# Threshold arithmetic in fewer GpSimd operations, two adjacency accumulators and other lags in a planned graph-network kernel

## The chip, the cores and the metric

The kernel runs on one core of a Trainium2 chip. The metric is the device time of one launch in microseconds; lower is better. Five engines work side by side: TensorE (PE in the profile), VectorE (DVE), ScalarE (ACT), GpSimd (POOL) and SyncE (SP), which issues nearly all transfers here.

## The reference, cut to what matters

Two graph layers over N = 3327 nodes with 256 features. Layer 0 makes two steps of two kinds of propagation. `R @ Xf` is a dense product with the row-normalised adjacency. `A @ Xa` uses attention whose rows are cut to the most probable entries that together hold 90% of the probability (top-p).

```python
h = maximum(layernorm(x), 0)                      # layer 0 works on h
R = adj + eye(N); R = R / R.sum(-1, keepdims=True)
Z = 0; Xf = Xa = h
for n in range(2):
    probs = softmax((Xa @ W1.T @ W2.T) @ (Xa @ W3.T).T)
    # keep an entry while the sum of the larger ones in its row is < 0.9
    A = probs * keep;  A = A / A.sum(-1)
    Xf = R @ Xf
    Xa = A @ Xa
    Z = Z + Xf @ U1[n].T + Xa @ U2[n].T
x = x + layernorm(h + Z)
h = maximum(layernorm(x), 0)
# layer 1: graph attention, 4 heads, masked by adj > 0
x = x + elu(softmax(where(adj > 0, leaky_relu(s_i + d_j), -inf)) @ (h @ W))
```

## The kernel before, in words

Nodes are cut into 26 tiles of 128 rows; all work on one tile of rows is a `Row`. Layer 0 is done in two steps, `n` = 0 and 1, and then comes layer 1's attention (`attend_neighbours`).

**One row of attention.** `search` lists its pieces. TensorE computes the logits (line 905), ScalarE their exponentials into a buffer `e` of 128 x 3327 (line 920), one of five. Then the threshold of the row is searched without sorting: ScalarE makes a first guess `t0` (`guess`, `density`, lines 940 to 950) and counts the whole row against it (`count`, line 957, one pass with Relu and one with Sign); GpSimd computes a better threshold from the sums (`step`, lines 965 to 1004), ScalarE counts again, and so on, two evaluations in step 1 and three in step 2 (`EVALS`). All numbers of the search are columns of a small tile `sc`, one number for each of the 128 rows. The last result `up` bounds a window of candidates: VectorE masks the row (line 1014), takes the eight largest of 16 pieces (line 1019), sorts and chooses (`sort`, `choose`), and sets everything under the threshold to zero in four pieces of at most 1024 columns (`drop`, line 1072). `total` on GpSimd gives the reciprocal of the row sum and writes a figure for a later check into `met[:, 4]`.

**From the row to the product.** For most rows VectorE transposes 32 x 32 blocks (line 1110), SyncE writes them to HBM (`put_blocks`) and reads them back in another order (`get_blocks`), and TensorE multiplies them (`attend_blocks`, line 1126). The last 128 columns are transposed by TensorE (`turn`, line 1085) right after the fourth drop. The last three rows of step 2 are all transposed that way (line 1103 is their product). The accumulator is `acca`, one bank of PSUM.

**The adjacency product.** `Full` streams the adjacency in (`load`, `at`), TensorE adds 26 matmuls into the accumulator `accf` (`some`, line 1151), and it is copied out: in step 2 scaled, by ScalarE (line 1162) or VectorE (line 1165).

**What sets the order.** Nothing is scheduled while the kernel runs. Each piece is declared to a planner with `plan.put(engine, length, rank, function, needs, take, give, lag, hold)`: its assumed duration, its priority (lower first), what it waits for, which named buffers it takes and gives back, how long after its end its result may be counted on[...]. `Plan.order` runs through these assumed times once, giving every free engine its ready piece of lowest rank. The program is written down in that order, so each engine's queue is fixed and in order; semaphores follow from the tiles that instructions read and write. An assumed duration or lag that is changed moves instructions on all queues.

Of the kernel before, what the change touches and what calls it, by code (L numbers as in the profile page):

```python
# [10 lines left out]
F32 = mybir.dt.float32  # L11
# [4 lines left out]
ALU = mybir.AluOpType  # L16
# [3 lines left out]
P = 128  # L20
# [567 lines left out]
def fast(  # L588
# [58 lines left out]
    with ExitStack() as l0:  # L647
# [218 lines left out]
        plan = Plan(dict(rows=1, mvs=3, pl=2, px=2, acca=1, accf=1, et=3, at=4, y=1, e2=3, mask=2, e5=1, qg=2, **BUFS))  # L866
# [4 lines left out]
        class Row:  # L871
# [3 lines left out]
                "b v w t0 t1 t2 u g k2 p0 p1 p2 p3 j0 j1 j2 j3 r0 s0 s1 s2 B0 B1 B2 q d dt least up h0 h1 room K zs nxt cnt "  # L875
                "tk rec".split()
# [68 lines left out]
            def density(self):  # L945

                S.activation(self.u, self.w, AF.Square, scale=math.sqrt(0.5))
                S.activation(self.u, self.u, AF.Exp)
                S.activation(self.b, self.s, AF.Copy, scale=1.0 - TOP_P)
                S.activation(self.k2, self.t0, AF.Square, scale=30.0)  # L950
# [8 lines left out]
            def step(self, k, eng):  # L959


                TS, TT = eng.tensor_scalar, eng.tensor_tensor
                t, tn, B = (self.t0, self.t1, self.t2)[k], (self.t1, self.t2, self.up)[k], (self.B0, self.B1, self.B2)[k]
                last = k + 1 == EVALS[self.n]

                def invert(x):
                    if eng is V:
                        V.reciprocal(x, x)
                    else:
                        TT(x, x, powers[:, 2:3], ALU.pow)  # L970

                s = (self.s0, self.s1, self.s2)
                if k == 0:
                    TS(self.q, s[0], float(N), t, ALU.add, ALU.mult)
                    TS(B, self.r0, -2.0, self.q, ALU.mult, ALU.add)
                else:
                    TS(self.v, t, (self.t0, self.t1)[k - 1], 0.5, ALU.add, ALU.mult)
                    TS(self.u, s[k], s[k - 1], self.v, ALU.subtract, ALU.mult)
                    TT(B, (self.B0, self.B1)[k - 1], self.u, ALU.add)
                TS(self.d, B, -0.5, self.b, ALU.mult, ALU.add)  # L980
                if k == self.n:

                    TS(self.least, s[k], N - 2.0 * (WIN[self.n] - 2), BIG, ALU.is_ge, ALU.mult)
                    TS(self.least, self.d, 0.0, self.least, ALU.is_ge, ALU.mult)
                if k == 0:
                    TS(self.g, self.u, cs[:, self.i : self.i + 1], 0.25, ALU.mult, ALU.min)
                elif last:
                    TT(self.w, self.k2, self.g, ALU.mult)
                    TS(self.w, self.u, self.dt, self.w, ALU.mult, ALU.add)
                    TS(self.v, self.u, self.u, self.k2, ALU.mult, ALU.add)  # L990
                    invert(self.v)
                    TT(self.g, self.w, self.v, ALU.mult)
                if k == 0 or last:
                    TS(self.q, self.g, 0.5, 1.0 / AIM[self.n], ALU.mult, ALU.add)
                    invert(self.q)
                TS(self.d, self.q, t, self.d, ALU.mult, ALU.add)
                TT(self.d, self.d, self.g, ALU.mult)
                if last:
                    TS(self.d, self.d, t, self.least, ALU.add, ALU.max)
                    TS(self.up, t, 0.25, self.d, ALU.mult, ALU.max)  # L1000
                else:
                    TT(self.d, self.d, t, ALU.add)
                    TS(tn, t, 0.25, self.d, ALU.mult, ALU.max)  # L1003
                    TS(self.dt, tn, t, 2.0, ALU.subtract, ALU.mult)
# [36 lines left out]
            def choose(self):  # L1041
# [22 lines left out]
                V.scalar_tensor_tensor(num, upto, self.m, num, ALU.is_le, ALU.mult, accum_out=self.tk)  # L1064
# [9 lines left out]
            def total(self):  # L1074

                GP.tensor_scalar(self.v, self.all, self.zs, self.rec, ALU.subtract, ALU.add)
                GP.tensor_tensor(self.rec, self.v, powers[:, 2:3], ALU.pow)
                GP.tensor_tensor(met[:, 4, self.i : self.i + 1], self.tk, self.m, ALU.subtract)
# [56 lines left out]
        class Full:  # L1135
# [11 lines left out]
            def some(self, js):  # L1147
                for j in js:
                    if j == 0:
                        self.acc = ps_a.tile([P, self.w], F32, name="accf")  # L1150
                    T.matmul(  # L1151
                        self.acc[:, : self.w], self.at[j // JC][:, j % JC, :], self.src[:, j, : self.w],
                        start=(j == 0), stop=(j == NT - 1),
                    )
# [35 lines left out]
        ready = []  # L1190
# [288 lines left out]
        def failures(n):  # L1479
# [14 lines left out]
            V.tensor_scalar(one, met[:, 4], 0.0, None, ALU.not_equal)  # L1494
# [7 lines left out]
        def search(row, rank, keys, stats_of, fresh):  # L1502
# [21 lines left out]
            more = plan.put("ACT", 0.55, rank - 2.2, row.density, needs=[a])  # L1524
            for j in range(2):
                got = [
                    plan.put("ACT", 3.05, rank - (2.1, 1.7)[j], row.count, j, fn, needs=[a])
                    for fn in (AF.Relu, AF.Sign)[j:]
                ]
                a = plan.put("POOL", (3.8, (4.7, 3.2)[n])[j], rank - (2.0, 1.6)[j], row.step, j, GP, needs=[got, more])  # L1530
            if EVALS[n] == 3:
                a = row.pieces["counted"] = plan.put("ACT", 3.05, rank - 1.4, row.count, 2, AF.Sign, needs=[a])
                a = plan.put("POOL", 4.3, rank - 1.3, row.step, 2, GP, needs=[a])
# [11 lines left out]
            total = plan.put("POOL", 1.2, rank - 1.0, row.total, needs=[a], give=["cum"])  # L1545
            drops = []
            for o in range(4):
                a = plan.put("DVE", 1.01, rank - 1.0, row.drop, o, needs=[a], hold=1.0)
                drops.append(a)
            return total, drops  # L1550

        def attention(row, rank, total, drops, right):
            a = None
            if row.i < BLOCKED[row.n]:
                come = []
                for g in range(3):
                    b = plan.put("DVE", 1.25, rank - 1.001, row.turn_blocks, g, needs=[drops[g]])
                    b = plan.put("SP", 0.5, rank - 1.0, row.put_blocks, g, needs=[b], lag=6.0)
                    b = plan.put("POOL", 0.02, -90.0, lambda: None, needs=[b], lag=0.0)
                    come.append(  # L1560
                        [plan.put("SP", 0.6, rank - 1.0, row.get_blocks, g, o, needs=[b], lag=4.5) for o in range(4)]
                    )
# [30 lines left out]
        def full(n, t, rank, right, after):  # L1593

            f = Full(n, t)
# [5 lines left out]
            for j in range(0, NT, 2):  # L1601
# [3 lines left out]
                    take=["accf"] * (j == 0), give=["at"] * last,  # L1605
                )
            if n == 1:
                a = plan.either(
                    ("ACT", 0.4, f.scaled_by_s), ("DVE", 0.45, f.scaled_by_v), -90.0, needs=[a], give=["accf"]
                )  # L1610
                b = plan.put("SP", 0.4, rank, f.fetch, needs=[loads[-1], stored[t]], take=["base"], lag=3.0)
# [497 lines left out]
```

## Time and profile before

| what | us |
|---|---|
| median of 3 runs | 2116.03 |
| lowest, highest | 2112.54, 2118.37 |
| profiled execution, its own time | 2116.11 |
| its span, first to last instruction | 2114.3 |
| TensorE busy in the span | 2044.3 |
| VectorE, ScalarE, GpSimd busy | 1732.8, 1285.1, 1073.9 |

The profile is of one execution. A name such as `PE accf L1151` is an engine, the tile written and the line of the kernel. A line of the waits, `A <- B: 9.6, 7, 3.7`, says that A stood still for B for 9.6 us in all, 7 times, at most 3.7 us at once. A group of instructions shows, after its shapes, how often it ran, its busy time and the mean of one in ns, and then the idle time ahead of it. A matmul of 32-bit numbers leaves two records in the trace, each 0.216 us apart for 256 columns.

### The profile page before, as it was taken

What the parts mean: (1) busy time and instruction counts of PE and PEld (TensorE: products, weight loads), DVE (VectorE), ACT (ScalarE), POOL (GpSimd) and SP (SyncE); (2) the same over time, 40 slices, a digit from 0 to 9 for tenths busy, and PEclk for the clock granted to TensorE, in tenths of its full rate; (3) what the DMA queues carried; (4) which work ended last, traced back from release to release, by engine and by line L of the source; (5) the groups of instructions that cost most, each with busy time, mean ns of one, the idle gap of its engine ahead of it and who ended that gap; (6) DMA issues with size and microseconds to landing.
All of it is one profiled execution on the core that took longest, in us unless ns stands there. A gap on an engine that the chain in (4) does not pass through costs nothing. (4 is left out here: it accounts for less than half of the span.)

```text
span 2114.3 us, 34595 instructions
## 1 busy us (share of the span) xinstructions
PE 2044.3 (97%) x10695; PEld 1414.4 (67%) x10695; DVE 1732.8 (82%) x4110; ACT 1285.1 (61%) x2371; POOL 1073.9 (51%) x2482
## 2 busy tenths in 40 slices
PE   8999999999999999999999999999999999999997
PEld 6477877877877888777777877878777333333332
DVE  5577998878887971569888989979787999999895
ACT  5676665566566612678677777767653547464552
POOL 4366675546565620568878888888883000000001
PEclk9999999999999999999999999999999999999999
DMA  3177978788876994787777887868763544454341
GB/s 96 44 187 176 194 194 193 168 170 183 188 177 166 205 207 129 217 182 181 182 177 166 190 194 177 199 158 198 160 153 91 165 140 140 119 153 117 110 127 34
DMA packets 580514, 338.57 MB, mean 160 GB/s; under 512 B 327930, under 2 KB 533280, under 8 KB 580320
## 3 DMA queue, kind: packets, MB, share of 16 engines
q1 hardware_dynamic: 579424, 336.06, 65.5%
q8 instruction: 87, 1.43, 0.3%
q14 instruction: 107, 0.88, 0.1%
q10 hardware_dynamic: 896, 0.21, 0.0%
HBM read 242.86 MB, written 93.05 MB: 159 GB/s over the span
## 5 line engine op out<-in xcount | busy, mean ns | idle before, releaser
L957 ACT ACTIVATE junk<-e,sc 128x3327 fp8e5<-128x3327 f32 x147 | 450.7, 3066 | 66.0 <-POOL sc L1003 64.5
L1126 PE MATMUL acca<-rhs,e 128*128 128x256 f32 x1872 | 423.9, 380 | 7.9 <-DMA e<-blocks 7.3
L1126 PEld LDWEIGHTS acca<-rhs,e 128*128 128x128 f32 x1872 | 364.1, 196 | 52.2 <-issue 13.0
L1151 PE MATMUL accf<-c,at 128*128 128x256 f32 x1352 | 318.9, 387 | 18.2 <-ACT main L1162 9.6
L1151 PE MATMUL accf<-main,at 128*128 128x257 f32 x1352 | 318.5, 384 | 6.2 <-DVE win L1036 4.0
L1151 PEld LDWEIGHTS accf<-c,at 128*128 128x128 f32 x1352 | 253.5, 192 | 70.0 <-ACT main L1162 12.4
L1151 PEld LDWEIGHTS accf<-main,at 128*128 128x128 f32 x1352 | 251.9, 191 | 59.2 <-issue 12.3
L1019 DVE MAX8 cands<-y 128x8 f32<-128x205 f32 (+1 forms) x832 | 243.1, 362 | 3.6
L1909 POOL TENSOR_TENSOR qq<-qq 128x256 f32<-128x256 f32 x4 | 3.0, 768 | 457.1 <-ACT qq L1905 457.0
L1014 DVE SCALAR_TENSOR_TENSOR y<-e,sc 128x1639 f32<-128x1639 f32 x84 | 165.1, 1965 | 57.6 <-POOL sc L1000 56.4
L1743 ACT ACTIVATE et<-at 128x448 bf16<-128x448 f32 (+1 forms) x204 | 112.2, 550 | 129.5 <-DVE e L1754 73.7
L1770 PE MATMUL pl<-e,main 128*64 128x416 f32 x1024 | 190.4, 517 | 0.1
L920 ACT ACTIVATE e<-pl 128x1024 f32<-128x1024 f32 (+1 forms) x168 | 152.0, 916 | 53.1 <-PE pl L905 51.5
L1072 DVE SCALAR_TENSOR_TENSOR e<-e,thr 128x1024 f32<-128x1024 f32 (+1 forms) x168 | 178.6, 1066 | 3.0 <-DMA kqs<-kq 0.5
L905 PE MATMUL pl<-kt,qg 64*128 64x512 f32 (+1 forms) x832 | 173.8, 536 | 0.0
L1110 DVE STREAM_TRANSPOSE e<-e 128x1024 f32<-128x1024 f32 x117 | 145.9, 1247 | 3.6
L1770 PEld LDWEIGHTS pl<-e,main 128*64 128x64 f32 x1024 | 70.3, 137 | 111.1 <-issue 92.2
L1754 DVE SCALAR_TENSOR_TENSOR e<-c,low,et 128x832 f32<-128x832 f32 x128 | 128.8, 1073 | 6.1 <-issue 3.2
L905 PEld LDWEIGHTS pl<-kt,qg 64*128 64x128 f32 x832 | 71.8, 186 | 83.9 <-issue 75.2
L1742 ACT ACTIVATE at<-at 128x448 f32<-128x448 f32 (+1 forms) x204 | 110.5, 541 | 25.3 <-DMA at<-in_adjt_dram 25.2
L1754 DVE SCALAR_TENSOR_TENSOR e<-qq,low,et 128x832 f32<-128x832 f32 x120 | 120.7, 1084 | 4.1 <-PE accf L1784 2.8
L957 ACT ACTIVATE junk<-qq,sc 128x3327 fp8e5<-128x3327 f32 x35 | 107.3, 3064 | 24.9 <-POOL sc L1003 24.8
(545 smaller groups left out, 3600.2 us busy)
## 6 DMA issues: line engine op xcount, KB each, us to landing
at<-in_adjt_dram SPq DMA_DIRECT2D x414, 256.0 KB
blocks<-e SPq DMA_DIRECT2D x117, 512.0 KB
e<-blocks SPq DMA_DIRECT2D x468, 128.0 KB
at<-in_adjt_dram SPq DMA_DIRECT2D x102, 192.0 KB
blocks<-qq SPq DMA_DIRECT2D x30, 512.0 KB
qq<-blocks SPq DMA_DIRECT2D x120, 128.0 KB
at<-in_adjt_dram SPq DMA_DIRECT2D x52, 128.0 KB
ys<-ystage SPq DMA_DIRECT2D x26, 256.0 KB
```

The lines of the kernel that those rows point to most:

```text
L905: T.matmul(pl[:, lo : lo + m], qg[self.n, self.i // 4][half, self.i % 4, :], kt[half, 512 * k : 512 * k + m], start=True, stop=True,)
L920: S.activation(to, pl, AF.Exp, accum_out=(self.p0, self.p1, self.p2, self.p3)[k],)
L957: S.activation(junk[:, :N], self.e[:, :N], fn, bias=t, scale=-1.0, accum_out=dst, saturate=False)
L1014: V.scalar_tensor_tensor(self.y[:, : hi - lo], self.e[:, lo:hi], self.up, self.e[:, lo:hi], ALU.is_lt, ALU.mult, accum_out=(self.h0, self. ...
L1019: V.max(self.cands[:, a * PIECES // 2 + k, :], self.y[:, at[k] - lo : at[k + 1] - lo])
L1072: V.scalar_tensor_tensor(piece, piece, self.thr[:, o : o + 1], piece, ALU.is_gt, ALU.mult)
L1110: V.transpose(part, part)
L1126: T.matmul(self.acc, lhs, rhs[self.n][:, j, :], start=(j == 0), stop=stop and j == js[-1])
L1151: T.matmul(self.acc[:, : self.w], self.at[j // JC][:, j % JC, :], self.src[:, j, : self.w], start=(j == 0), stop=(j == NT - 1),)
L1743: S.activation(to, src, AF.Sign)
L1754: V.scalar_tensor_tensor(held["e"][:, k, :], extra["both"][b % 2][:, k, :], low[:, j, k : k + 1], held["mask"], ALU.max, ALU.mult,)
L1770: T.matmul(q["acc"][a][k * FH : (k + 1) * FH, c, :C], main[:, j, h * FH : (h + 1) * FH], held["e"][:, h, c * C : (c + 1) * C], start=(j == 0),
```

## The change

`step(k)` is split. `before(k)` computes on GpSimd what doesn't need the count that is running (`g`, `h`, `x`, `mid`, floors of the result); `step(k)` does the rest. Halves and signs are moved into constants, so that some operations fall away, ScalarE makes two more small ones in `density` (`th`, `tq`), and the two reciprocals of the last evaluation are one operation on two neighbouring columns `v`, `z`. The comparison that `total` made for each row is made once for all rows in `failures`. The pieces get other assumed lengths.

In step 2 the adjacency accumulator becomes one tile of 512 columns, of which even and odd tiles of rows use a half each; the planner is told of two buffers, `fa` and `fb`.

For the planner the first three drops last 1.07 us and the fourth 0.4 (before 1.01 each), what follows the fourth may come 1.5 us after it (before 0.15), and blocks read back are counted on after 5.5 us (before 4.5).

```diff
             def density(self):
...
-                S.activation(self.k2, self.t0, AF.Square, scale=30.0)
+                S.activation(self.k2, self.t0, AF.Square, scale=15.0)
+                S.activation(self.th, self.t0, AF.Copy, scale=-0.5)
+                S.activation(self.tq, self.t0, AF.Copy, scale=0.25)
...
-            def step(self, k, eng):
...
-                if k == 0:
-                    TS(self.q, s[0], float(N), t, ALU.add, ALU.mult)
-                    TS(B, self.r0, -2.0, self.q, ALU.mult, ALU.add)
-                else:
-                    TS(self.v, t, (self.t0, self.t1)[k - 1], 0.5, ALU.add, ALU.mult)
-                    TS(self.u, s[k], s[k - 1], self.v, ALU.subtract, ALU.mult)
-                    TT(B, (self.B0, self.B1)[k - 1], self.u, ALU.add)
-                TS(self.d, B, -0.5, self.b, ALU.mult, ALU.add)
-                if k == self.n:
...
-                    TS(self.least, s[k], N - 2.0 * (WIN[self.n] - 2), BIG, ALU.is_ge, ALU.mult)
-                    TS(self.least, self.d, 0.0, self.least, ALU.is_ge, ALU.mult)
+            def before(self, k):
...
                 if k == 0:
                     TS(self.g, self.u, cs[:, self.i : self.i + 1], 0.25, ALU.mult, ALU.min)
-                elif last:
-                    TT(self.w, self.k2, self.g, ALU.mult)
-                    TS(self.w, self.u, self.dt, self.w, ALU.mult, ALU.add)
+                    TS(self.h, self.g, 0.5, 1.0 / A, ALU.mult, ALU.add)
+                    TT(self.h, self.h, powers[:, 2:3], ALU.pow)
+                    TT(self.x, self.h, t, ALU.mult)
+                    return
+                TS(self.mid, t, ts[k - 1], -0.25, ALU.add, ALU.mult)
+                if k + 1 < EVALS[n]:
+                    TT(self.x, self.h, t, ALU.mult)
+                    TS(self.tq, t, 0.25, None, ALU.mult)
+                else:
+                    TS(self.dh, ts[k - 1], t, 0.5, ALU.subtract, ALU.mult)
+                    TS(self.kh, self.k2, self.g, 0.5, ALU.mult, ALU.mult)
+                    TS(self.fl, ss[n], N - 2.0 * (WIN[n] - 2), BIG, ALU.is_ge, ALU.mult)
+                    TS(self.fl, Ds[n], 0.0, self.fl, ALU.is_ge, ALU.mult)
+                    TS(self.fl, t, 0.25, self.fl, ALU.mult, ALU.max)
+
+            def step(self, k):
...
+                if k == 0:
+                    TS(self.mid, s[0], float(N), self.th, ALU.add, ALU.mult)
+                    TS(D, self.mid, self.r0, self.b, ALU.add, ALU.add)
+                else:
+                    TS(self.u, s[k], s[k - 1], self.mid, ALU.subtract, ALU.mult)
+                    TT(D, (self.D0, self.D1)[k - 1], self.u, ALU.add)
+                if k + 1 < EVALS[self.n]:
+                    TS(d, D, self.x, self.g, ALU.add, ALU.mult)
+                    TS((self.t1, self.t2)[k], d, t, self.tq, ALU.add, ALU.max)
+                else:
                     TS(self.v, self.u, self.u, self.k2, ALU.mult, ALU.add)
-                    invert(self.v)
-                    TT(self.g, self.w, self.v, ALU.mult)
-                if k == 0 or last:
-                    TS(self.q, self.g, 0.5, 1.0 / AIM[self.n], ALU.mult, ALU.add)
-                    invert(self.q)
-                TS(self.d, self.q, t, self.d, ALU.mult, ALU.add)
-                TT(self.d, self.d, self.g, ALU.mult)
-                if last:
-                    TS(self.d, self.d, t, self.least, ALU.add, ALU.max)
-                    TS(self.up, t, 0.25, self.d, ALU.mult, ALU.max)
-                else:
-                    TT(self.d, self.d, t, ALU.add)
-                    TS(tn, t, 0.25, self.d, ALU.mult, ALU.max)
-                    TS(self.dt, tn, t, 2.0, ALU.subtract, ALU.mult)
+                    TS(self.w, self.u, self.dh, self.kh, ALU.mult, ALU.add)
+                    TS(self.z, self.v, 1.0 / A, self.w, ALU.mult, ALU.add)
+                    k = self.NAMES.index("v")
+                    both = self.sc[:, k : k + 2]
+                    TT(both, both, powers[:, 2:3].to_broadcast([P, 2]), ALU.pow)
+                    TT(self.x, t, self.z, ALU.mult)
+                    TS(d, D, self.v, self.x, ALU.mult, ALU.add)
+                    TS(d, d, self.w, 2.0, ALU.mult, ALU.mult)
+                    TS(self.up, d, t, self.fl, ALU.add, ALU.max)
...
             def total(self):
...
-                GP.tensor_tensor(met[:, 4, self.i : self.i + 1], self.tk, self.m, ALU.subtract)
...
             def some(self, js):
                 for j in js:
                     if j == 0:
-                        self.acc = ps_a.tile([P, self.w], F32, name="accf")
+                        if self.n == 0 or self.t == 0:
+                            pair[0] = ps_a.tile([P, 512], F32, name="accf")
+                        lo = 0 if self.n == 0 else self.t % 2 * D
+                        self.acc = pair[0][:, lo : lo + self.w]
...
-            more = plan.put("ACT", 0.55, rank - 2.2, row.density, needs=[a])
-            for j in range(2):
-                got = [
-                    plan.put("ACT", 3.05, rank - (2.1, 1.7)[j], row.count, j, fn, needs=[a])
-                    for fn in (AF.Relu, AF.Sign)[j:]
+            more = plan.put("ACT", 0.95, rank - 2.2, row.density, needs=[a])
+            b = plan.put("POOL", 1.7, rank - 2.0, row.before, 0, needs=[more])
+            last = EVALS[n] - 1
+            for j in range(last + 1):
+                r = rank - (2.0, 1.6, 1.3)[j]
+                a = [
+                    plan.put("ACT", 3.05, r - 0.1, row.count, j, fn, needs=[a])
+                    for fn in ((AF.Relu, AF.Sign) if j == 0 else (AF.Sign,))
                 ]
-                a = plan.put("POOL", (3.8, (4.7, 3.2)[n])[j], rank - (2.0, 1.6)[j], row.step, j, GP, needs=[got, more])
-            if EVALS[n] == 3:
-                a = row.pieces["counted"] = plan.put("ACT", 3.05, rank - 1.4, row.count, 2, AF.Sign, needs=[a])
-                a = plan.put("POOL", 4.3, rank - 1.3, row.step, 2, GP, needs=[a])
+                if j == 2:
+                    row.pieces["counted"] = a
+                a = plan.put("POOL", 1.55 if j < last else 4.1, r, row.step, j, needs=[a, b])
+                if j < last:
+                    b = plan.put("POOL", 2.3 if j + 1 == last else 1.15, r + 0.1, row.before, j + 1, needs=[a])
...
-            total = plan.put("POOL", 1.2, rank - 1.0, row.total, needs=[a], give=["cum"])
+            total = plan.put("POOL", 1.0, rank - 1.0, row.total, needs=[a], give=["cum"])
             drops = []
             for o in range(4):
-                a = plan.put("DVE", 1.01, rank - 1.0, row.drop, o, needs=[a], hold=1.0)
+                a = plan.put(
+                    "DVE", 1.07 if o < 3 else 0.4, rank - 1.0, row.drop, o, needs=[a], hold=1.0 if o < 3 else 0.3,
+                    lag=0.15 if o < 3 else 1.5,
+                )
                 drops.append(a)
...
-                        [plan.put("SP", 0.6, rank - 1.0, row.get_blocks, g, o, needs=[b], lag=4.5) for o in range(4)]
+                        [plan.put("SP", 0.6, rank - 1.0, row.get_blocks, g, o, needs=[b], lag=5.5) for o in range(4)]
...
-            f = Full(n, t)
+            f, mine = Full(n, t), ["accf"] if n == 0 else [("fa", "fb")[t % 2]]
...
-                    take=["accf"] * (j == 0), give=["at"] * last,
+                    take=mine * (j == 0) + ["accf"] * (n == 1 and t == j == 0), give=["at"] * last,
...
             if n == 1:
                 a = plan.either(
-                    ("ACT", 0.4, f.scaled_by_s), ("DVE", 0.45, f.scaled_by_v), -90.0, needs=[a], give=["accf"]
+                    ("ACT", 0.4, f.scaled_by_s), ("DVE", 0.45, f.scaled_by_v), -90.0, needs=[a], give=mine
                 )
```

## The prediction

> **What bounds the kernel now.** The page comes first: its busy line tells which engine has no room left.
>
> ```profile
> span 2114.3 us, 34595 instructions
> ...
> PE 2044.3 (97%) x10695; PEld 1414.4 (67%) x10695; DVE 1732.8 (82%) x4110; ACT 1285.1 (61%) x2371; POOL 1073.9 (51%) x2482
> ```
>
> TensorE is the bound, so the time is its work plus its idle time, 2114.3 - 2044.3 = 70.0 us. Its matmuls are the same after the change (5585 TensorE instructions in both built programs), so only those 70 us can move. The table by windows says where they lie: step 1 is about 95 to 860 us, step 2 860 to 1610, the layer-1 attention the rest.
>
> ```profile
> 860.00:1610.00 750.00, 710.85 (x3294) 568.25 (x3291) 641.32 (x1759) 523.15 (x849) 592.24 (x1346) 0.99 0.76 179
> 95.00:860.00 765.00, 755.45 (x3485) 601.80 (x3487) 591.86 (x1635) 444.04 (x757) 423.82 (x984) 1.00 0.78 180
> ```
>
> The second column is TensorE: it idles 750 - 710.85 = 39.2 us in step 2 and 9.6 us in step 1; some 21 us lie in the start and the last stage, which the diff hardly touches. GpSimd (the sixth) is 79% busy in step 2 and 55% in step 1. So the change is worth what it does to 39 us, and the waits of TensorE between 860 and 1610 us name them (total, times, longest):
>
> ```profile
> PE accf L1151 <- ACT main L1162: 9.6, 7, 3.7
> PE px L1085 <- DVE e L1072: 7.8, 8, 2.1
> PE acca L1126 <- DMA e<-blocks: 7.3, 10, 1.5
> PE accf L1151 <- DMA at<-in_adjt_dram: 5.6, 3, 3.8
> PE accf L1151 <- DVE main L1165: 3.0, 2, 2.4
> ```
>
> These five are 33.3 us. The change aims at four of them: the finished adj accumulator being copied out (9.6 + 3.0 = 12.6 us in 9 waits), the last drop before a transpose (7.8), and blocks coming back from HBM (7.3). Only the adjacency load (5.6) is not addressed. Two more waits in the same window show how threshold arithmetic reaches the others: ScalarE's counts and VectorE's windows wait for its last operation.
>
> ```profile
> ACT junk L957 <- POOL sc L1003: 48.5, 27, 6.9
> ...
> DVE y L1014 <- POOL sc L1000: 41.2, 11, 7.9
> ```
>
> Neither engine is full, so these cost time only where they make a copy or a drop late.
>
> [...] operations on one number per partition take 0.3 to 0.6 us, so on GpSimd the number of instructions is the cost.
>
> **Part 1, the arithmetic.** Three groups carry the prices (mean ns of one after the busy time):
>
> ```profile
> L970 POOL TENSOR_TENSOR sc<-sc,powers 128x1 f32<-128x1 f32 x156 | 98.2, 629 | 13.0
> L996 POOL TENSOR_SCALAR sc<-sc 128x1 f32<-128x1 f32 x130 | 68.4, 526 | 13.9
> ...
> L980 POOL TENSOR_SCALAR sc<-sc 128x1 f32<-128x1 f32 x130 | 42.2, 324 | 13.6
> ```
>
> In step 2 a row has 11, 11 and 15 operations after its three counts. Adding the means of their lines in that window gives 4.25 + 4.33 + 6.26 = 14.8 us; the planner assumed 3.8 + 3.2 + 4.3 = 11.3. After, 4 + 4 + 10 operations follow a count, by the same rows 1.6 + 1.7 + 4.5 = 7.8 us, and 4 + 3 + 6 run while ScalarE counts (3.07 us a count): 1.5 + 1.1 + 2.4 = 5.0. Together 12.8 us, where the new plan assumes 12.35. The power of two numbers at once is not in the trace; 0.63 us for one and 0.99 for four (L851) bound it, and I take 0.75. GpSimd has 312 instructions fewer in all (2170 for 2482, one for each row in `total`), about 62 us less in step 2 and 45 in step 1. TensorE gets none of this directly. What it gets is a plan whose order is off by 0.4 us a row on GpSimd instead of 3.5, so ScalarE and VectorE keep their places better. I take 2 us in step 2 (an eighth of the 12.6 us of copies that come late), between 0 and 8, and 1 us in step 1.
>
> ScalarE pays two operations more a row at 0.19 us (as L949 and L950), 52 x 0.38 = 20 us. They stand ahead of the row's counts, which start 0.4 us later; ScalarE is idle 227 of 750 us in step 2, so I cost them at nothing. Without that cover they would come behind copies TensorE waits for, at most 10 us in step 2.
>
> **Part 2, two accumulators.** Both halves are columns of one tile in one bank, and the built order shows what becomes of that. In 16 of 25 changes of tile, matmuls of the next tile (mostly a pair of blocks) now stand before the copy of the finished one. But the copy waits for that pair, and the pair after it waits for the copy: the wait is not gone, it has moved 0.87 us into the next tile (4 records of 0.216 us). Counting what stands on TensorE between the matmul that releases the copy and the one that waits for it: nothing in 9 cases before and in 10 after; in 5 more of after only two to four small matmuls or transposes. Queued behind the waiting matmul is everything on TensorE, logits of the next rows too. Before, a bare change cost 12.6 / 9 = 1.4 us. After, the copy itself (0.47 us) is the least a bare one can cost; but a ScalarE that comes late has 0.87 us of grace. I take 0.9 us for ten and 0.3 for five: 10.5 us, **2 us less** than 12.6. The ends are 10 x 0.47 = 4.7 us (8 less) and 15 x 1.4 = 21 us (8 more).
>
> **Part 3, later drops and loads.** No instruction is added. The plan gives the drops 3 x 1.07 + 0.4 us and then 1.5 us before the last transpose may follow, 5.1 us; before it was 4 x 1.01 + 0.15 = 4.2. The trace has 1.25 us for each of the three large drops and 0.44 for the small one, 4.2 us. So transposes move 0.9 us later behind other matmuls, against waits of 1.0 us on average and 2.1 at most: if these spread evenly from 0 to 2.1 us, (1.2 / 2.1) squared = a third is left. **5 us less** of 7.8. The block loads are assumed 1.0 us later, against waits of 0.7 on average and 1.5 at most: by the same reckoning a tenth is left, **6 us less** of 7.3, if the queue of SP, which issues puts, block loads and adjacency loads in one order, does not fall behind. The 468 + 120 block loads move later in it, past adjacency loads, which come no later for it. A row keeps its buffer 1 us longer of some 144 (five buffers, 28.8 us a row), which costs nothing. What is late next is the adjacency load, 5.6 us.
>
> **The sum.** A new order makes waits of its own; I allow 3 us (nothing to 10). Then -2 - 1 - 2 - 5 - 6 + 3 = -13 us. The profiled execution took 2116.1 us around its span of 2114.3, as good as the median of 2116.0. **2103 us.**
>
> **The rivals.** *No change, about 2113 us.* VectorE is 641 of 750 us busy in step 2, and the plan believes in 3.6 us of drops where the trace has 4.2. It falls behind 0.6 us a row, where it was 0.16, and eats the 0.9 us given. Then parts 1 to 3 leave some 3 us. For it: `DVE y <- POOL`, which shows it waiting already. Against: these waits shrink with 7 us less arithmetic on a row's path.
>
> *Slower, about 2128 us.* The copies. A copy on ScalarE stands in line behind counts of 3.07 us, and now TensorE has already been committed to the next tile when it finds out. At 2.4 us for each of the 15 thinly covered changes they cost 36 us instead of 12.6, +23, and the rest of the sum, without the 2 of part 2, is -11: +12. This decides from some 1.6 us a change (24 us, 11 more than before: the rest's gain is used up). For it: the longest copy wait of 3.7 us. Against: the 1.4 us average, and a ScalarE less often held by GpSimd.
>
> *Much faster, about 2091 us.* With threshold operations off the path, all four addressed waits go almost entirely: 12.6 + 7.8 + 7.3 = 27.7, less 3 for new ones. For it: the waits of 48.5 and 41.2 us. [...] That the change does not do what it says holds for its second part, by the built order, and is in the sum already.
>
> **How the numbers follow.** About 0.3%, 6.3 us, is what a measurement of this kernel can tell from no change. The forecast has 0.47, much faster 0.13, no change 0.20, slower 0.20. Faster is 0.60, same 0.20, slower 0.20. The range runs from 2086 us (all 27.7 us of the addressed idle time gone, and 2 of the rest) to 2126 (15 x 2.25 = 34 us of copy waits, 21 more, against -11).
>
> **What would show it.** GpSimd busy near 960 us; TensorE idle in step 2 near 27 us; the waits for L1072 and for blocks together under 5 us; waits of adj matmuls for the copies still there, around 10 us, but in the middle of a tile. It is wrong if the copy waits are gone or above 20 us, if transposes still wait 7 us for drops, or if step 1 loses what step 2 gains.

## The result, and the profile after

The changed kernel takes as long as the one before: 2114.53 us against 2113.88 (medians of 12 runs each), ratio 0.9999 with a 95% interval of 0.999 to 1.0008. The forecast was 2103. The profiled execution took 2113.02 us around a span of 2111.2.

The busy line of the page after, with its span:

```profile
span 2111.2 us, 34313 instructions
...
PE 2041.5 (97%) x10695; PEld 1414.9 (67%) x10695; DVE 1728.0 (82%) x4108; ACT 1297.9 (61%) x2477; POOL 993.5 (47%) x2170
```

GpSimd works 80 us less. TensorE idles 2111.2 - 2041.5 = 69.7 us, where it was 70.0. The table by windows of the changed kernel, step 2 and then step 1 (sum, then TensorE, its weight loads, VectorE, ScalarE, GpSimd, granted clock, DMA share, GB/s):

```profile
860.00:1610.00 750.00, 717.21 (x3323) 577.00 (x3322) 640.82 (x1761) 530.70 (x901) 544.24 (x1174) 0.99 0.77 180
95.00:860.00 765.00, 749.71 (x3462) 596.45 (x3463) 587.02 (x1617) 446.59 (x806) 391.61 (x845) 1.00 0.78 179
```

Idle time of TensorE in step 2 fell from 39.2 to 32.8 us, and in step 1 it rose from 9.6 to 15.3. Nearly all that step 2 gained, step 1 lost. The waits of TensorE in step 2 of the changed kernel (total, times, longest; L1156 is the adj matmul, L1087 the transpose after the fourth drop, L1128 the product of blocks):

```profile
PE accf L1156 <- DMA at<-in_adjt_dram: 9.2, 6, 4.5
PE px L1087 <- ACT et L1098: 5.4, 1, 5.4
PE accf L1156 <- ACT main L1167: 4.5, 8, 0.6
PE pl L905 <- ACT e L920: 3.1, 1, 3.1
PE acca L1128 <- DMA e<-blocks: 2.7, 5, 0.8
PE accf L1156 <- DVE main L1170: 2.3, 4, 1.0
PE px L1087 <- DVE e L1075: 2.1, 3, 0.9
```

The waits that the change aims at did fall: copies 4.5 + 2.3 = 6.8 us (12.6 before), drops 2.1 (7.8), blocks 2.7 (7.3), together 11.6 for 27.7. None of them is over 1 us at once any more. But other single waits stand high in the list: one of 5.4, one of 3.1, and loads of up to 4.5. A fourth heads the waits of step 1 (95 to 860 us):

```profile
PE px L1087 <- ACT ystage L1350: 7.7, 2, 6.8
```

The two longest, of 6.8 and 5.4 us, can be followed to a transfer. At 740.3 us VectorE writes the last part of a `ystage` tile; SyncE issues its store only at 743.7, behind twelve block loads and four adjacency loads, and ScalarE can't overwrite the tile until the store has landed, at 751.2. That copy would have freed the PSUM tile that TensorE's transpose needs. Who waited for whom is in the answer for the tile `ystage`, 725 to 756 us:

```profile
L1361 SPq DMA_DIRECT2D ys<-ystage x1: 385/385/385, 743.7 to 743.7; - x1
L1350 ACT COPY ystage<-px x1: 587/587/587, 751.2 to 751.2; 128x512 f32<-128x512 f32 x1
...
  ACT ystage L1350: 9.4, 1
  PEld px L1087: 7.2, 1
  PE px L1087: 6.8, 1
```

The planner counts such a store as done 3.0 us after its issue; this one took 7.5.

The wait of 5.4 us stands at the end of step 2. There ScalarE begins layer 1's masks (line 1741) ahead of copies that TensorE needs. Its waits between 1580 and 1600 us:

```profile
ACT kt L1741 <- DMA kt<-in_adjt_dram: 6.3, 1, 6.3
```

The first mask needs the first two of these loads. They were issued at 1575.6 and 1576.1 us and are planned with 4.0; the mask starts at 1585.9, 9.8 us after the second was issued. The answers for the loads (1576 to 1577 us) and for the masks:

```profile
L1734 SPq DMA_DIRECT2D kt<-in_adjt_dram x2: 456/772/1089, 1575.6 to 1576.1; - x2
L1741 ACT ACTIVATE kt<-kt x2: 882/890/897, 1585.9 to 1587.7; 128x832 f32<-128x832 f32 x2
```

**What a long wait costs besides itself.** The same place by windows of 2 and 4 us (the last three columns are the granted clock, the DMA share and GB/s):

```profile
1584.00:1588.00 4.00, 0.56 (x3) 0.15 (x1) 0.21 (x1) 2.04 (x3) 0.00 (x0) 1.00 0.75 220
1588.00:1590.00 2.00, 0.00 (x0) 0.00 (x0) 2.00 (x3) 1.97 (x4) 0.00 (x0) 0.60 0.02 9
1590.00:1594.00 4.00, 4.00 (x12) 3.37 (x13) 3.96 (x11) 0.44 (x1) 0.00 (x0) 0.50 0.00 0
1594.00:1596.00 2.00, 2.00 (x9) 1.64 (x8) 1.84 (x6) 0.59 (x1) 0.24 (x1) 0.70 0.07 24
1596.00:1600.00 4.00, 4.00 (x21) 3.51 (x20) 3.93 (x11) 0.37 (x1) 3.18 (x6) 1.00 0.06 21
```

TensorE stops at 1584.6. Within 4 us the clock falls to 0.50, and it stays there until 5 us after work has begun again: 12 matmul records in 4 us, then 21. Another 4.00 x 0.50 + 2.00 x 0.30 = 2.6 us are lost while the engine counts as busy. At 752 us it is 1.8; there TensorE stops at 745.0 and works again from 751.9:

```profile
748.00:750.00 2.00, 0.00 (x0) 0.00 (x0) 0.00 (x0) 0.00 (x0) 0.00 (x0) 0.68 0.80 202
750.00:752.00 2.00, 0.14 (x1) 0.14 (x2) 0.00 (x0) 0.78 (x2) 0.11 (x1) 0.50 0.05 17
752.00:754.00 2.00, 2.00 (x6) 1.69 (x7) 1.41 (x2) 2.00 (x1) 1.92 (x3) 0.50 0.00 0
754.00:756.00 2.00, 2.00 (x7) 1.63 (x6) 1.97 (x3) 0.87 (x2) 1.57 (x3) 0.62 0.00 0
```

Worked out from the windows of both places, half speed began 3.8 us after the stop at 1584.6 and 3.7 after the one at 745.0, and ended 5.2 and 3.7 us after the restart. So the wait of 5.4 us cost 8.0. Other stops in these runs went otherwise (last section). The half speed lasted 6.8 us at both places; the longer stop lost less because 3.1 us of that time had passed before work began again, against 1.6 at the other.

In the kernel before such losses lie at 96, 908 and 1144 us, after stops of 4.0, 3.8 and 3.7 us. The last of these is a wait for a copy, which the change did remove, with the 2.4 us that the clock lost there:

```profile
PE accf L1151 <- ACT main L1162: 3.7, 1, 3.7
1144.00:1150.00 6.00, 4.50 (x11) 3.57 (x12) 5.17 (x17) 5.91 (x6) 4.67 (x11) 0.50 1.22 222
```

In no other slice of 2 us from 90 to 1700 us was its clock under 0.9, so the many waits of around 1 us had no such loss. The changed kernel has three more besides the two above: at 908 (1.4 us lost, after a load waited for 4.5 us), 1052 (1.4, after the wait of 3.1 us) and 1226 (1.7, after waits of 1.7 and 0.6 us close together). Summed over slices of 2 us from 90 to 1700 us, the clock cost 8.4 us of busy time before and 8.9 after. Long waits cost more than themselves on both sides, so the clock hardly moves the balance.

### The profile page after: what moved, and what is told of

Read it like the earlier page. It is cut to its first block, busy times and chain, and to the rows that moved or that the text cites. A ratio compares the mean times of both kernels' runs of the same rounds, so it can differ in the third digit from the quotient of the medians.

```text
span 2111.2 us, 34313 instructions
## 1 busy us (share of the span) xinstructions
PE 2041.5 (97%) x10695; PEld 1414.9 (67%) x10695; DVE 1728.0 (82%) x4108; ACT 1297.9 (61%) x2477; POOL 993.5 (47%) x2170
## 5 line engine op out<-in xcount | busy, mean ns | idle before, releaser
L1128 PE MATMUL acca<-rhs,e 128*128 128x256 f32 x1872 | 427.4, 381 | 3.7 <-DMA e<-blocks 2.7
L1128 PEld LDWEIGHTS acca<-rhs,e 128*128 128x128 f32 x1872 | 364.5, 197 | 48.5 <-issue 8.1
L1156 PE MATMUL accf<-c,at 128*128 128x256 f32 x1352 | 317.0, 386 | 16.0 <-DMA at<-in_adjt_dram 9.2
L1156 PE MATMUL accf<-main,at 128*128 128x257 f32 x1352 | 313.3, 381 | 5.1 <-ACT main L1307 2.5
L1156 PEld LDWEIGHTS accf<-c,at 128*128 128x128 f32 x1352 | 252.2, 191 | 68.1 <-DMA at<-in_adjt_dram 12.2
L1156 PEld LDWEIGHTS accf<-main,at 128*128 128x128 f32 x1352 | 250.5, 190 | 54.1 <-issue 11.3
L1757 ACT ACTIVATE at<-at 128x448 f32<-128x448 f32 (+1 forms) x204 | 110.8, 543 | 27.7 <-DMA at<-in_adjt_dram 27.5
```

What stands on the lines that cost most here:

```text
L1128: T.matmul(self.acc, lhs, rhs[self.n][:, j, :], start=(j == 0), stop=stop and j == js[-1])
L1156: T.matmul(self.acc[:, : self.w], self.at[j // JC][:, j % JC, :], self.src[:, j, : self.w], start=(j == 0), stop=(j == NT - 1),)
```

## The experiments

Three theories stood against each other. **Places**: the gain was made and then lost at single places where the planner's lag is too short. **Orders**: any new order scatters by about what was gained, and the result says little of the change. **VectorE's pace**: step 2 ends when VectorE's rows do. Every time below is a median, and the ratio, with its 95% interval, is against runs of the kernel before on the same chip. On the chips used, the kernel before ran at 2112.3 to 2115.3 us, so in tables that set times from several chips side by side, differences of some 3 us say nothing.

**One part alone, on the kernel before.** Each adds the hunks of one part to it: part 1 (e1, `density`, `before`, `step` and their pieces), part 2 (e2), part 3 (e3). The edits of e2 and e3, cut (e2 also has the planner's two buffers `fa` and `fb`, which move the order):

```diff
-                        self.acc = ps_a.tile([P, self.w], F32, name="accf")
+                        if self.n == 0 or self.t == 0:
+                            pair[0] = ps_a.tile([P, 512], F32, name="accf")
+                        lo = 0 if self.n == 0 else self.t % 2 * D
+                        self.acc = pair[0][:, lo : lo + self.w]
```

```diff
-                a = plan.put("DVE", 1.01, rank - 1.0, row.drop, o, needs=[a], hold=1.0)
+                a = plan.put(
+                    "DVE", 1.07 if o < 3 else 0.4, rank - 1.0, row.drop, o, needs=[a], hold=1.0 if o < 3 else 0.3,
+                    lag=0.15 if o < 3 else 1.5,
+                )
...
-                        [plan.put("SP", 0.6, rank - 1.0, row.get_blocks, g, o, needs=[b], lag=4.5) for o in range(4)]
+                        [plan.put("SP", 0.6, rank - 1.0, row.get_blocks, g, o, needs=[b], lag=5.5) for o in range(4)]
```

> The kernel before with the new threshold arithmetic and its plan lengths alone (one accumulator, old lags of drops and block loads). Theory A (each part does what it aims at in step 2, and new waits at single places in the new order take it back): no more than 0 to 5 us faster than before from this part; TensorE idle between 860 and 1610 us stays at 35 to 40 us, since the three waits of 7.8, 7.3 and 12.6 us are not addressed; GpSimd busy near 990 us. Theory B (the waits are elastic: VectorE, 85% busy, or the transfers give the pace, so what is removed in one place comes up in another): same time within 3 us, whatever happens to the single waits. Theory C (the arithmetic is what gains, the accumulators or the lags lose): 8 to 15 us faster.

Measured: 2120.08 us, ratio 1.0024 (1.0009 to 1.004).

> The kernel before with the two halves of one accumulator bank in step 2 alone. In the kernel after, the matmuls' waits for the copies fell from 12.6 us in 9 waits to 6.8 us in 12. Theory A: the same here, the copy waits fall by some 6 us to 6 or 7 us, and the time by 3 to 6 us, unless one new wait of several us appears at one place. Theory B: the copy waits fall but the idle time of TensorE in step 2 stays within 3 us of 39, and the time within 3 us. Theory C: 3 to 10 us slower.

Measured: 2105.97 us, 0.9957 (0.9944 to 0.997).

> The kernel before with the later drops and block loads alone. Theory A: waits for the drops fall from 7.8 to about 2 us and those for blocks from 7.6 to about 3 us in step 2, 10 us together; the time falls by 5 to 10 us, unless single new waits appear. Theory B: those two fall as said, but TensorE's idle time in step 2 stays within 3 us of 39. Theory C: slower by 3 to 10 us, with the new waits in step 1 (there 9.6 us idle before, 15.3 after).

Measured: 2128.3 us, 1.0066 (1.0053 to 1.0078).

**An order redrawn, on the kernel before.** The count of 3.07 us is assumed 3.06 instead of 3.05, here and at the third count, which is not shown. Few lines of TensorE's order move.

```diff
-                    plan.put("ACT", 3.05, rank - (2.1, 1.7)[j], row.count, j, fn, needs=[a])
+                    plan.put("ACT", 3.06, rank - (2.1, 1.7)[j], row.count, j, fn, needs=[a])
```

> The kernel before with one assumed length changed by next to nothing: a count is 3.06 us for the planner instead of 3.05 (the trace has 3.07). No instruction is added or removed, 29 lines of TensorE's order differ. It measures how far a new order of the same work moves the time. Theory A: within 3 us of before, and the waits in the same places, as so few instructions move. Theory B: within 3 us too. A rival to all (the result of any change here is mostly a draw of the order): more than 3 us either way.

Measured: 2116.33 us, 1.0007 (0.9997 to 1.0017).

**One part taken out of the changed kernel**: the lags (e6), the accumulators (e7), the arithmetic (e8). The edits are the hunks above turned round.

> The kernel after with the old lags and lengths of drops and block loads (arithmetic and two accumulators stay). Alone, the arithmetic took 5 us and the accumulators gained 9, the lags lost 13. Theory A: the waits at the end of step 1 for the store of a staged tile (7.7 us in the kernel after) come from the lags; they shrink to 2 or 5 us, and the time is 2104 to 2111 us, although the waits for drops and blocks come back by part. Theory B: the time is that of before within 3 us. If the parts added up, it would be 4 us faster than before.

Measured: 2126.1 us, 1.0059 (1.0042 to 1.0077).

> The kernel after with one accumulator in step 2 (arithmetic and lags stay). The accumulators alone gained 9 us. Theory A: they gain in this order too, so 4 to 10 us slower than after, with waits for the copies of 8 to 13 us in step 2 instead of 6.8. Theory B: as after within 3 us. If the parts added up, 18 us slower than before.

Measured: 2098.4 us, 0.993 (0.9913 to 0.9947).

> The kernel before with the accumulators and the lags. Alone, the one gained 9 and the other lost 13 us: if they added up, 4 us slower than before. Theory A: between before and 8 us slower, the loss of the lags at the end of step 1 (7 us idle there) stays, as the accumulators touch step 2 alone. Theory B: within 3 us of before.

Measured: 2125.39 us, 1.0059 (1.0037 to 1.0082).

The three parts in all combinations, in us:

| | no lags | lags |
|---|---|---|
| neither | 2113.9 | 2128.3 |
| accumulators | 2106.0 | 2125.4 |
| arithmetic | 2120.1 | 2098.4 |
| both | 2126.1 | 2114.5 |

They do not add. The arithmetic costs 6 and 20 us without the lags and brings 30 and 11 with them. The accumulators bring 8 and 3 without the arithmetic and cost 6 and 16 with it. No sum over the parts gives such a table. e6 shows what happens where the lags are missing: TensorE's waits of e6, 1580 to 1640 us.

```profile
PE px L1087 <- DVE e L1075: 15.8, 2, 8.9
```

In e6 VectorE's last drop ends at 1634.9 us (1611.2 in the changed kernel). TensorE has no adj matmul left by then and stands still for 8.9 and 6.9 us; in the changed kernel 28 adj records still come after VectorE's last drop. The adj matmuls are the stock that covers late rows. That is VectorE's pace deciding, in this order. Why VectorE's last rows come 24 us later in e6 was not followed up.

**The late masks.** The changed kernel, with one lag corrected:

```diff
-                        loads, own = plan.put("SP", 0.2, rank, load_first, needs=[opened[0]], lag=4.0), []
+                        loads, own = plan.put("SP", 0.2, rank, load_first, needs=[opened[0]], lag=12.0), []
```

> The kernel after with the first two adjacency loads of layer 1 counted on 12 us after their issue instead of 4 (they landed more than 10 us after it), so that the two masks they feed leave their place ahead of copies that TensorE waits for at 1590 us (one wait of 5.4 us); 14 lines of TensorE's order differ. Theory A (gains of the middle given back at single places): that wait goes, 3 to 6 us faster than after, so 2108 to 2111 us, and TensorE idle from 1560 to 1630 us falls from 5.9 to about 2. Theory B (elastic waits): the idle time there stays, as the last rows wait for VectorE all the same; within 2 us of after.

Measured: 2104.46 us, 0.996 (0.9945 to 0.9976), 10 us under the changed kernel. Few lines of TensorE's order move. The last 70 us of step 2, changed kernel first, then e5:

```profile
1560.00:1630.00 70.00, 64.09 (x313) 55.26 (x312) 54.31 (x152) 24.38 (x43) 33.30 (x56) 0.95 0.32 95
```

```profile
1560.00:1630.00 70.00, 68.96 (x356) 56.83 (x358) 57.16 (x160) 29.17 (x52) 34.61 (x60) 1.00 0.38 115
```

4.9 us of idle time are gone and the clock is back at 1.00, which is 2.6 us more: 7.5 of the 10. TensorE's records in the window rise by 43, at 0.216 us each 9.3 us of work. The wait for the masks is no longer in the list. This place is shown.

**Two more orders of the pair that differs by the accumulators, the masks without them, and the copies told later.** e9 is e7 with e5's edit. e10 and e12 assume the count at 3.06 us, with the accumulators and without. e11 is the changed kernel with one more argument for the last two adj matmuls of a tile of step 2:

```diff
                     take=mine * (j == 0) + ["accf"] * (n == 1 and t == j == 0), give=["at"] * last,
+                    lag=1.0 if n == 1 and j == NT - 2 else None,
```

> The changed kernel without the two accumulators, and with layer 1's mask loads assumed 12 us long for the planner (4 before). If single places given a wrong length cost the same wherever they stand, the two gains add: 16 us (accumulators) and 10 us (masks), 2088 us. If what counts is TensorE's idle time in the last 70 us of layer 0, 3.7 us without the accumulators against 5.9 with them, at most 3 us are to be had: 2095 to 2098 us, with about 1 us idle left there. If the gains are the luck of one order, anything from 2090 to 2110 us.

Measured: 2099.99 us, 0.9934 (0.9919 to 0.995): nothing gained on e7. In e7 ScalarE's masks hold up no copy that TensorE needs, so there was nothing to gain. The costs of places do not add either. It also means that the 16 us between e7 and the changed kernel contain the wait for the masks: between e9 and e5, which both are without it, the accumulators cost 4 us.

> The changed kernel with each count assumed 3.06 us long instead of 3.05, a difference without meaning that draws another order (some 300 lines of TensorE's order differ). If the parts of the change have costs of their own, within 4 us of the changed kernel: 2110 to 2118 us, with about 30 to 35 us of TensorE's idle time in step 2. If much of what the earlier runs showed is the luck of one order, 2100 or 2125 us are as likely.

Measured: 2104.14 us, 0.9958 (0.9943 to 0.9974), also 10 us under the changed kernel, from a figure without meaning. But not without a cause. Waits of e10 in step 1:

```profile
PE px L1087 <- ACT ystage L1350: 4.9, 2, 3.7
```

The wait of 6.8 us is one of 3.7 here, step 1 ends at 857.4 us instead of 864.4, and these 7 us are kept to the end (the last product of layer 1 is at 2085.7 us instead of 2093.5). The late masks are in e10 too, 5.1 us. It is the changed kernel with one of its two longest waits cut to about half, and 2.6 us less idle time in step 2.

> The changed kernel, two accumulators included, but the planner lets the copy of a finished tile come 1.0 us after the tile's last matmuls instead of 0.15, about the 0.87 us of the next tile's pair [...]. If the accumulators cost 16 us because the copies stand waiting on ScalarE and VectorE ahead of the rows' work (19.5 and 8.4 us in step 2), those two waits fall under 15 us together and the time falls by about 10 us, to 2104. If it is TensorE's wait for the copies that costs, it grows instead (6.8 us in step 2 now) and the time stays or rises, 2114 to 2120 us. By luck of the order, anything within 10 us of 2114.

Measured: 2097.47 us, 0.9931 (0.9916 to 0.9947). 17 us are gained, but not as the theory has it. ScalarE's and VectorE's waits of e11 in step 2:

```profile
ACT main L1167 <- PE accf L1156: 15.6, 11, 3.8
```

```profile
DVE main L1170 <- PE accf L1156: 10.2, 6, 4.0
```

They are 25.8 us, hardly less than 27.9. That copies standing in line cost the 16 us is not shown. What is gone from TensorE's waits in step 2 of e11 is the 5.4 us for the masks and the 3.1 us for one exponential, two single waits that its edit does not name; step 2 idles 23.3 us there instead of 32.8. The new order is without them.

> The changed kernel without the two accumulators, and with each count assumed 3.06 us long. If the accumulators themselves cost some 16 us in the changed kernel, this stays within 4 us of 2098 and some 14 us under the redrawn changed kernel that runs beside it. If the 16 us were the luck of two orders, the difference of this pair is anything from -10 to +10 us.

Measured: 2093.22 us, 0.9898 (0.9881 to 0.9915), 11 us under its partner e10. Over the six pairs that differ by the accumulators alone (e2 to before, e6 to e1, e8 to e3, changed to e7, e10 to e12, e5 to e9) the effect is -8, +6, -3, +16, +11, +4: on average +4, with a standard error of 4. What the accumulators are worth stays open.

**Four orders of each kernel.** The count assumed 3.02 and 3.08 us, in the kernel before (e13, e14) and in the changed one (e15, e16).

> The kernel before with each count assumed 3.02 us long instead of 3.05: nothing changes but the order that is drawn (about a thousand lines of TensorE's order differ). If the order before is a typical one, within 5 us of 2114. If orders of this planner scatter by 10 us and more whatever the change, it may be 2100 or 2125 us as well, and then the prediction's error is within what a draw does.

Measured: 2117.89 us, 1.0028 (1.0018 to 1.0037).

> The kernel before with each count assumed 3.08 us long: a second draw, same reading. With the kernel itself and the earlier redrawn order this makes four orders of before.

Measured: 2101.99 us, 0.9944 (0.9931 to 0.9957).

> The changed kernel with each count assumed 3.02 us long. If the change is worth some 10 us in itself and its own order was an unlucky one (2114 us, the redrawn one 2104), this lies near 2104 and under both redrawn orders of before that run beside it. If the change is worth nothing, it scatters about 2114 as they do.

Measured: 2098.63 us, 0.9927 (0.9915 to 0.994).

> The changed kernel with each count assumed 3.08 us long: a second draw, same reading. With the kernel itself and the earlier redrawn order this makes four orders of the changed kernel.

Measured: 2091.01 us, 0.99 (0.9886 to 0.9914).

The idle times are TensorE's, 95 to 860 and 860 to 1630 us:

| count | before: us | step 1 | step 2 | after: us | step 1 | step 2 |
|---|---|---|---|---|---|---|
| 3.05 | 2113.9 | 9.5 | 39.1 | 2114.5 | 15.3 | 32.8 |
| 3.06 | 2116.3 | 10.9 | 42.5 | 2104.1 | 10.4 | 30.2 |
| 3.02 | 2117.9 | 10.3 | 40.1 | 2098.6 | 7.2 | 27.9 |
| 3.08 | 2102.0 | 4.1 | 36.3 | 2091.0 | 10.0 | 23.7 |
| mean | 2112.5 | 8.7 | 39.5 | 2102.1 | 10.7 | 28.7 |

Orders scatter by 7 us (before) and 10 us (after), standard deviations. The means differ by -10.4, with a standard error of 6: likely a gain, not a firm one. Step 2 is firmer: every order of the changed kernel idles less than every order of before, by 10.8 us on average with a standard error of 2.3. The order that was measured is the worst of four. The best of them, e16, by windows:

```profile
860.00:1630.00 770.00, 746.32 (x3554) 596.05 (x3555) 679.00 (x1816) 544.05 (x938) 553.17 (x1169) 1.00 0.77 182
```

It has no wait over 4.4 us left, and its clock costs 3.2 us of busy time by the same sum over slices that gave 8.9 for the changed kernel and 8.4 before.

**The store, and all of it together.** e17 gives the store of y in step 1 the lag it needs:

```diff
-                y = plan.put("SP", 0.5, r + 0.3, store, needs=[a], give=["ystage"], lag=3.0)
+                y = plan.put("SP", 0.5, r + 0.3, store, needs=[a], give=["ystage"], lag=8.0)
```

> The changed kernel, with the stores of y in step 1 counted by the planner as done 8 us after they are issued (3 before). If the 7 us that TensorE loses at 745 to 752 us come from that store alone and nothing later gives them back, step 1 ends near 857 us instead of 864 and the time is near 2107. If the end of step 2 is set by VectorE's rows whatever step 1 does, the gain is gone by then: 2114. The order is drawn anew as well, which by the eight orders measured may add or take 10 us.

Measured: 2096.81 us, 0.9921 (0.9904 to 0.9937). The wait for `ystage` is gone from step 1, which ends at 848.3 us; at the end of step 2 a new one stands. Windows of step 1, then the waits of 1560 to 1630 us:

```profile
95.00:860.00 765.00, 760.70 (x3530) 607.09 (x3531) 595.61 (x1630) 452.48 (x815) 393.67 (x853) 1.00 0.80 184
```

```profile
PE px L1087 <- DVE e L1075: 8.2, 1, 8.2
```

Step 1 gained 16 us, over twice what was expected, and the whole gain was kept: e17 is 17.7 us under the changed kernel. So the second reading, that it would be gone by the end, is refuted as a forecast of the time. The wait that it foresaw did come: the last drop was only 9 us sooner (1602.1 for 1611.2), and TensorE, further ahead of the rows, stood 8.2 us for it, where the changed kernel had stood 5.4 us for the masks. The whole order was drawn anew with this edit, so how much of the gain is the store's alone is not shown.

e18 has the edits of e5 and e11, and the count at 3.06.

> The changed kernel with three of the planner's figures changed together: the copy of a finished tile 1.0 us after its last matmuls, layer 1's mask loads 12 us, counts 3.06 us. If each of the three removes its own wait, 17 + 10 + 10 us add up: 2077. If masks and copies act on the same idle time at the end of step 2 (as masks gave nothing without the accumulators), about 2088 to 2092. By luck of the order alone, 2090 to 2105.

Measured: 2087.7 us, 0.9883 (0.9865 to 0.9902), the fastest of all kernels here. The sum of three gains, 2077, is missed by 11 us. The time fits a shared piece of idle time: e11 had already lost its wait for the masks, so the 10 us of e5 could not be had twice. A lucky order (2090 or a little less) would fit nearly as well. Windows of e18:

```profile
860.00:1630.00 770.00, 750.41 (x3577) 598.74 (x3580) 670.52 (x1811) 547.50 (x942) 548.08 (x1170) 1.00 0.77 182
```

Idle time in step 2 is 19.6 us, half of before.

## Why the prediction was wrong, point by point

- **The arithmetic** was priced well for a row: 12.9 us of GpSimd measured in step 2, 12.8 forecast; the power of two numbers takes 0.72 us (median; 0.75 taken). GpSimd's busy time came to 993.5 us, not 960: the old operations took 14.5 us a row in the trace, not 14.8, and 48 and 32 us fell off in steps 2 and 1 where I had 62 and 45. ScalarE's two operations cost nothing to be seen.
- **Copies, drops, blocks.** Forecast -2, -5, -6; with the arithmetic's -2 on the copies, -15 in step 2. Measured -5.8, -5.7, -4.6: **-16.1**. As forecast, records of the next tile stand ahead of 16 of the 25 copies (the one at 918.0 us waits 0.97 us for TensorE's records, and TensorE then 0.57 us for it). The copies were better than the 2 us that Part 2 was thought to gain, and in e7, without the accumulators, they wait 8.5 us, little more than 6.8. So, in these orders, most of that gain is not part 2's.
- **The step that failed** is the last term: "A new order makes waits of its own; I allow 3 us (nothing to 10)." In this order step 2 gave back 16.1 - 6.4 = 9.7 us and step 1 another 5.7, **15.4 us** in all. The waits account for it: 7.0 us more for the store in step 1, and in step 2 3.5 more behind a mask load, 3.1 for one exponential, 3.6 more for adjacency loads. That is 17.2; against it, a wait of 4.0 us at the start of step 1 became one of 2.5. The wait for the store is in step 1, where I had counted on 1 us less; "if step 1 loses what step 2 gains" was named as the sign of failure, and that is what happened.
- **Why it was mis-sized.** I listed the waits that the change removes and the lags that it corrects, and did not ask which other lags were as wrong. The lags of the store (3.0 us, where 7.5 passed) and of the mask loads (4.0, where 9.8 passed) were the same in the kernel before; there they happened to hold up little (0.7 and 1.9 us). In the new order they held up 7.7 and 5.4. Whether that is because the engines keep closer to the plan, or because any other order meets these lags elsewhere, is not shown; e10, where a figure without meaning halved one of the two, speaks for the second.
- **One order for a mean.** The sum of -13 is near the mean of four orders, -10.4, and -12 for step 2 (-2 - 2 - 5 - 6 + 3) nearer still to the -10.8 measured. A single order lies 7 to 10 us off its mean. The range, 2086 to 2126, allowed for that. One of the four orders, the measured one, lies within 6.3 us of the kernel before, which does not speak against the 0.20 given to no change.
- **The rivals.** No change came true, but by luck and not for its reason: VectorE's drops, which were to come late again, are waited for 2.1 us. The slower rival, TensorE waiting for copies for 36 us, is refuted at 6.8. Much faster (2091) is the time that e16 reaches in another order, with adjacency loads, which the change does not address, as its largest wait. Halves in two tiles, each in a bank of its own, were not tried in any run here; whether a copy waits for the next pair because of the bank or because of the one tile is not shown.
- **The parts are not separable.** Arithmetic and lags each lose alone and, without the accumulators, win together. The contrast, some -33 us on average, is nearly three standard deviations of what the scatter of orders gives (about 12), but it was picked out after the table was seen. By what path they need each other was not settled.

## What to carry to other kernels

In a kernel with an order fixed ahead, sum what a change removes, but quote the sum as a mean over orders. Before believing one measured order, draw three more with a meaningless change of one assumed time, for both kernels, and compare the idle time stage by stage. Then list the longest single waits, not only the largest totals: each may be one lag to correct, and a stop can cost the clock as well: here one of 3.1 us cost 1.4 us more, one of 5.4 us 2.6.

## What the runs showed of the hardware

- After stops of 5.4 and 6.8 us TensorE's clock was granted at 0.50 for 6.8 us, and came back 5.2 and 3.7 us after the restart, with 2.6 and 1.8 us of work lost. The length of the stop alone does not decide it: in the changed kernel it fell after a stop of 3.1 us (0.57 from 1052 to 1056 us), and in e8 it stayed at 1.00 after one of 3.6 us. The clock is the last column but two:

```profile
1052.00:1056.00 4.00, 3.25 (x10) 1.87 (x11) 3.81 (x14) 3.52 (x9) 3.40 (x9) 0.57 1.13 186
```

```profile
PE accf L1154 <- DMA at<-in_adjt_dram: 3.6, 1, 3.6
920.00:928.00 8.00, 4.43 (x24) 2.82 (x20) 7.25 (x36) 7.87 (x15) 4.35 (x15) 1.00 0.74 203
```

- Such losses summed to 3.2 us in e16 and 12.8 in e6. TensorE was busy 2034.6 and 2049.4 us in these two runs, with the same 10695 records; the clock is 9.6 of the 14.8 us between them.
- Two transfers came 9.8 and 7.5 us after their issue. For most of the second, the store, the DMA engines were at 90% or more: busy tenths from 725 to 752 us, in 40 slices. The store was issued in the 28th and landed in the 39th. From the 37th on the engines were nearly idle, so what held its last 1.9 us, from 749.3 to 751.2, is not explained by full engines.

```profile
DMA  9609946939999879999999999999999999992000
```
